# Two expert layers and an attention on one core: pairs of pages and fetches in two written orders, one picked on chip by the counts

## The chip, the cores and the metric

The kernel runs on one core of one Trainium2 chip. The metric is the device time of one execution in microseconds. The core has TensorE (PE, with its weight loads shown apart as PEld), VectorE (DVE), ScalarE (ACT), GpSimd (POOL) and SyncE (SP), which issues most DMAs. Each engine works through its own instruction queue in order and waits on semaphores for the others. A software DMA is one that POOL issues with a list of row numbers (an indirect DMA); each such instruction here moves 128 rows of 256 floats, 131 KB.

## The reference, cut to what matters

The input is x, 4 x 1024 tokens of 256 floats. Four blocks follow one another, each on a layernorm of x and added to it:

```
x = x + rwkv(layernorm(x))          # recurrence over time, per batch entry
x = x + ffn(layernorm(x))           # "layer 1" below
x = x + retention(layernorm(x))     # attention with 16 heads and a decay
x = x + ffn(layernorm(x))           # "layer 2": the same weights

def ffn(x):                          # 4096 tokens, 64 experts, width 64
    logits = x @ router_w
    scores = softmax(logits)
    topk_idx = top_k(logits + router_bias, 4)
    w = scores at topk_idx, divided by their sum
    routed = sum over the 4 picked e of w[e] * (silu(x @ wg[e]) * (x @ wu[e])) @ wd[e]
    shared = sum over 2 of (silu(x @ swg[s]) * (x @ swu[s])) @ swd[s]
    return routed + shared
```

Which expert a token picks depends on the data. The 16384 picks fill pages of 128 rows, every page for one expert; how many pages are in use after so and so many tokens is known only when the kernel runs.

## The kernel before, in words

The tokens are cut into 8 segments of 512 (`xs[i]`, held in SBUF throughout), two segments per batch entry. All work is written as lists of small steps. `track(steps, lo, hi)` gives the steps of one list evenly spread due times from lo to hi, and `merge` sorts the steps of several lists by due time and emits them; that fixes the order on each engine's queue, and a unit of due time is one pair of pages (below).

Stage 1 computes the recurrence per segment. `route(i)` has two halves. The `choose` steps (norm, logits, pick, rank, place, weigh) normalise segment i, pick experts and give each pick a row in a page; `place` keeps running page counts in `upto`. The `send` steps issue 16 indirect DMAs on POOL (L402) that write each token's normalised row to its four places in the DRAM tensor `sent`. `shared(i)` is the shared expert of segment i: TensorE L426 and L439, ACT L431, DVE L432 and L444. `plan()` works out, from `upto`, which expert owns each page. `sent` is cleared to zeros at the start, and so are the rows of `made` from pair 82 on (3584 KB, L162 to L167).

`routed()` works on pairs of pages. `step(p)` loads pair p on SP (L489: rx, 256 KB of `sent`; L491: two rw of 192 KB, the weights of the two pages' experts) and computes earlier pairs: `up(p-2)` transposes rx (L501, DVE copy L505), `mid(p-3)` does gate and up projections (L513, ACT L518, DVE L521, ACT L522), `down(p-4)` the last product (L532) and writes `made` from ACT's queue (L539). `gather(i)` brings the results of segment i back: four `fetch` steps, each of four indirect DMAs on POOL (L562), and four `add` steps, each of four DVE instructions (L573) that add the rows times their weight to `xs[i]`. The adds come LAG = 7 units after their fetches, in program order on DVE.

A fetch of segment i may run once all the pages that segment i can lie in are made. `pairs_until(i)` is the most pairs that can be in use after segment i, in the worst case of the counts: 40, 48, 56, 64, 72, 80, 88, 96. Gather i is due at `pairs_until(i) + 3.5`. MOST = 82 pairs are always computed. The other 14 are computed only if the counts need them: `rest()` loads the count into registers on all engines and puts pairs 82 to 95 in a `tc.If` (L474). Segments 6 and 7, whose `pairs_until` is above 82, are fetched behind all that, as are all steps due at 86 or later.

In layer 1 the attention runs beside the pairs: `batch(b)` is batch entry b, 41 steps over 24 units from 54 + 24 b (FIRST = 54). So entry 0 and a third of entry 1 lie before the `rest()` of layer 1 and the others behind it, together with the last gathers of layer 1 and layer 2's routes 0 to 5, two per entry, at `max(86, 54 + 24 (b + 1))` and 12 later; shared experts 0, 1 and 2 of layer 2 follow their routes (BESIDE = 3). Then come routes 6 and 7 with shared 3 and 4 as fill, layer 2's `plan()`, the pairs of layer 2 with shared 5, 6 and 7 beside them, the gathers of segments 0 to 4 and a part of segment 5, `rest()`, and the remaining gathers. As each segment is complete, SP stores it (L1146).

The pools: `xnT` (transposed normalised segments for shared experts) has 5 buffers in layer 2; `pg`, the buffers of layer 1's fetches (tag gy, 4 of them, 6 in layer 2), is held on the left to the end of the attention. Steps that the text below uses are at L392 (the exponential of the weights in `weigh`, ACT), L983, L1002 and L1006 (attention).

## Time and profile before

| what | value |
|---|---|
| median of 5 runs | 1744.22 us |
| lowest, highest | 1742.79, 1750.87 us |
| the profiled execution's own time | 1744.35 us |
| its span in the trace | 1742.6 us (1.75 us lie around it) |
| mean clock granted to TensorE | 0.88 |
| busy: PE, PEld, DVE, ACT, POOL | 1366.5, 960.9, 1021.6, 707.0, 511.5 us |
| stage 1 | 0 to about 453 us |
| layer 1's pairs | first on TensorE at 457.3 us |
| layer 1's `rest()`, skipped | TensorE's branch at 841.5 us |
| last routes (segments 6, 7) | from about 1325 us |
| layer 2's pairs | first on TensorE at 1393.1, last write of `made` issued at 1674.2 us |
| layer 2's `rest()`, skipped | TensorE's branch at 1673.2 us |
| last of 256 fetches of both layers | 1733.5 us |

How to read it: "busy" is the time in which an engine has at least one instruction at work. In a row of groups, "idle before" is the engine's idle time ahead of the group's instructions, and after "<-" stands what ended most of it. The 40 slices of the page are 43.6 us each; a digit is the busy share in tenths.

### The profile page before, as it was taken

The numbers are of one execution on the slowest core, as the hardware profiler recorded it, in microseconds if no ns is written. First come the engines' busy times: TensorE is split into PE (matmuls) and PEld (weight loads), VectorE is DVE, ScalarE is ACT, GpSimd is POOL, SyncE is SP. The second block draws the span as 40 slices with busy tenths as digits, with TensorE's granted clock in tenths as the row PEclk, the third lists the DMA queues.
The fourth block names the chain that finished last, engine by engine and source line by source line (L and its number), as shares of the span: only waits on it lengthen the run. The fifth ranks groups of instructions, "written<-read, shape, count | busy, mean of one in ns | idle before, by whom it ended". The sixth has DMA issues, their size and how long they took to land. (4 is left out here: it accounts for less than half of the span.)

```text
span 1742.6 us, 24370 instructions
## 1 busy us (share of the span) xinstructions
PE 1366.5 (78%) x8264; PEld 960.9 (55%) x8264; DVE 1021.6 (59%) x2447; ACT 707.0 (41%) x1364; POOL 511.5 (29%) x528
## 2 busy tenths in 40 slices
PE   5597999977588799989866977969689299988830
PEld 2264555554477566767532654647546178776720
DVE  5887899985255454666544842537356255554643
ACT  5675777632134443565321422224232044444310
POOL 0025043453300422231354131031130600054566
PEclk8799999988799988999776978979899699999955
DMA  9949611121699944563322010010010499999944
GB/s 367 386 144 183 176 49 49 49 87 60 231 330 335 341 155 143 177 220 96 97 75 71 22 50 27 1 49 19 31 49 7 143 307 314 327 320 310 310 154 126
DMA packets 192955, 278.15 MB, mean 160 GB/s; under 512 B 53684, under 2 KB 119095, under 8 KB 192823
## 3 DMA queue, kind: packets, MB, share of 16 engines
q1 hardware_dynamic: 144630, 166.34, 30.2%
q0 software_dynamic: 24576, 67.14, 11.8%
q10 hardware_dynamic: 23616, 43.00, 6.5%
q8 instruction: 71, 1.16, 0.3%
q14 instruction: 62, 0.50, 0.1%
HBM read 164.74 MB, written 124.26 MB: 166 GB/s over the span
## 5 line engine op out<-in xcount | busy, mean ns | idle before, releaser
L402 POOL DMA_INDIRECT sent<-xn_f,to_f x256 | 263.5, 1029 | 635.5 <-ACT w_f L392 249.0
L562 POOL DMA_INDIRECT gy_f<-made,to_f x256 | 245.2, 958 | 578.7 <-DMA rw_f<-wx 266.0
L513 PE MATMUL rg_f<-rxT_f,rw_f 128*128 128x128 f32 x1312 | 191.7, 291 | 14.6 <-DMA rw_f<-wx 4.3
L513 PEld LDWEIGHTS rg_f<-rxT_f,rw_f 128*128 128x128 f32 x1312 | 170.4, 202 | 25.1 <-DVE rxT_f L505 11.6
L505 DVE COPY rxT_f<-rt_f 128x512 f32<-128x512 f32 x164 | 112.9, 689 | 113.4 <-PE rt_f L501 86.2
L501 PE MATMUL rt_f<-ident,rx_f 128*128 128x128 f32 x656 | 110.8, 295 | 68.5 <-DMA rx_f<-sent 53.7
L532 PE MATMUL rp_f<-rw_f,rh_f 64*128 64x128 f32 x1312 | 146.1, 306 | 19.9 <-issue 6.4
L439 PE MATMUL o_f<-f_swd,sh_f 128*128 128x256 f32 x512 | 131.1, 406 | 23.4 <-DVE x L444 14.3
L573 DVE SCALAR_TENSOR_TENSOR x<-gy_f,w_f,x 128x256 f32<-128x256 f32 x256 | 120.9, 481 | 46.8 <-DMA gy_f<-made,to_f 41.2
L426 PE MATMUL u_f<-xnT_f,f_swu 128*128 128x512 f32 x256 | 128.4, 621 | 14.6 <-DVE pm L983 11.4
L532 PEld LDWEIGHTS rp_f<-rw_f,rh_f 64*128 64x128 f32 x1312 | 109.8, 193 | 49.4 <-issue 15.6
L426 PE MATMUL g_f<-xnT_f,f_swg 128*128 128x512 f32 x256 | 133.5, 639 | 3.1 <-DVE pm L983 1.5
L538 ACT COPY ry_f<-rp_f 128x256 f32<-128x256 f32 x248 | 88.2, 373 | 115.7 <-PE rp_f L532 48.0
L518 ACT ACTIVATE rs_f<-rg_f 64x256 f32<-64x256 f32 x164 | 61.5, 375 | 167.4 <-PE rg_f L513 109.7
L501 PEld LDWEIGHTS rt_f<-ident,rx_f 128*128 128x128 f32 x656 | 76.7, 148 | 92.6 <-DMA rx_f<-sent 49.8
L439 PEld LDWEIGHTS o_f<-f_swd,sh_f 128*128 128x128 f32 x512 | 101.1, 204 | 47.7 <-DVE x L444 16.7
L983 DVE TENSOR_TENSOR pm<-sc,decay 128x512 f32<-128x512 f32 x128 | 83.9, 684 | 56.9 <-remote 28.4
L521 DVE TENSOR_TENSOR rh_f<-rg_f,rs_f 64x256 f32<-64x256 f32 x164 | 69.9, 426 | 71.2 <-ACT rs_f L518 45.8
L1006 ACT COPY retT<-rp 128x256 f32<-128x256 f32 x32 | 11.9, 373 | 217.4 <-remote 116.2
L641 PE MATMUL rvk<-xnT_a,rvk 128*128 128x512 f32 x192 | 92.4, 623 | 1.0 <-DVE xnT_a L220 0.6
L426 PEld LDWEIGHTS u_f<-xnT_f,f_swu 128*128 128x128 f32 x256 | 49.5, 199 | 74.1 <-issue 58.1
L431 ACT ACTIVATE sh_f<-g_f 128x512 f32<-128x512 f32 x64 | 37.9, 597 | 116.3 <-PE g_f L426 76.5
(227 smaller groups left out, 2352.5 us busy)
## 6 DMA issues: line engine op xcount, KB each, us to landing
rw_f<-wx SPq DMA_DIRECT2D x328, 192.0 KB
rx_f<-sent SPq DMA_DIRECT2D x164, 256.0 KB
made<-ry_f ACTq DMA_DIRECT2D x164, 256.0 KB
sent<-zeros SPq DMA_DIRECT2D x7, 2048.0 KB
sent<-zeros SPq DMA_DIRECT2D x1, 10240.0 KB
x<-in_x_dram SPq DMA_DIRECT2D x8, 512.0 KB
wx<-in_wg_dram SPq DMA_DIRECT2D x2, 2048.0 KB
sent<-xn_f,to_f POOLq DMA_INDIRECT x256
```

What stands on the lines that cost most here:

```text
L402: ins = nc.gpsimd.indirect_dma_start(out=rows_sent[: pairs_until(i) * 2 * P, :], out_offset=bass.IndirectOffsetOnAxis(ap=st["to"][:, c : c ...
L426: nc.tensor.matmul(ps, lhsT=w[:, k, s], rhs=self.xnT[i][:, k, :], start=(k == 0), stop=(k == KC - 1),)
L439: nc.tensor.matmul(o[:, t, :], lhsT=st["h"][:, c, s], rhs=self.weights[2][:, c, :], start=(c == 0), stop=(c == NS - 1),)
L501: nc.tensor.transpose(tp[:, k, j, :], s["x"][:, j, k * P : (k + 1) * P], ident)
L505: nc.vector.tensor_copy(out=xT, in_=tp)
L513: nc.tensor.matmul(gu[:, j, :], lhsT=s["w"][:, j, k * 2 * F : (k + 1) * 2 * F], rhs=s["xT"][:, k, j, :], start=(k == 0), stop=(k == KC - 1),)
L532: nc.tensor.matmul(yp[:, j, :], lhsT=s["h"][r, j, :], rhs=s["w"][r, j, WD:], start=True, stop=True,)
L538: copy(out=y[:, :, c * P : (c + 1) * P], in_=yp)
L562: nc.gpsimd.indirect_dma_start(out=y[:, k, :], out_offset=None, in_=rows_made[: ready[t] * 2 * P, :], in_offset=bass.IndirectOffsetOnAxis( ...
L573: tc.keep_in_program_order(nc.vector.scalar_tensor_tensor(out=xs[i][:, t, :], in0=got[t][:, k, :], scalar=s["w"][:, c : c + 1], in1=xs[i][ ...
L641: nc.tensor.matmul(ps, lhsT=rvk[:, k, lo : lo + P], rhs=st["xnT"][:, k, :], start=(k == 0), stop=(k == KC - 1),)
L983: nc.vector.tensor_mul(out=pm, in0=ch[j]["sc"][g], in1=decay.rearrange("p (k g b) n -> p g k b n", k=KC, b=2)[:, g],)
```

## The change

- MOST, `rest()`, FIRST and ROUTE go. A second list of limits, `USUAL[i]` = 33, 38, 43, 51, 59, 67, 75, 83 pairs, stands beside `pairs_until`. `plan()` compares the page counts after each segment with 2 * `USUAL` (66, 76, 86, 102, 118, 134, 150, 166 pages; eight memsets at the start make that table) and counts how many segments exceed their limit.
- `in_order(arm)` loads that number on all engines. If it is 0, the arm written with `USUAL` runs; else the arm written with `pairs_until`. Both are in the program.
- An arm of layer 1 holds all pairs (83 with `USUAL`, 96 else), all eight gathers at `until(i) + 3.5`, and batch entries 0 and 1 from `until(0) + 14` on (47 to 71 and 71 to 95 with `USUAL`). Behind it come entry 2 with routes 0 to 3 of layer 2, 6 units apart, and entry 3 with routes 4 and 5, 12 apart; shared experts 0 and 1 follow their routes (BESIDE = 2).
- Routes 6 and 7 now have three shared experts as fill (2, 3 and 4; FILL = 3).
- An arm of layer 2 holds all pairs, all eight gathers at `until(i) + 3.5` and the stores, shared 5 and 6 from 0.5 to n - 4 and shared 7 from n - 3 to n + 11, where n is the number of pairs.
- With `USUAL`, segment 6's gather is due at 78.5 and segment 7's at 86.5, behind 83 pairs.
- `xnT` of layer 2 has 7 buffers instead of 5. `pg` moves to the right side, in the inner stack, which closes when layer 1's arm is over. The rows of `made` are no longer cleared.

```diff
--- before.py
+++ after.py
@@ -71,7 +71,8 @@
     NPAIR = (NPAGE + 1) // 2
 
 
-    MOST = min(NPAIR, (N * TOPK // P + E // 2 + 4) // 2)
+
+    USUAL = [(max(E + 2 + 10 * i, (i + 1) * SEG * TOPK // P + E // 2 + 6) + 1) // 2 for i in range(NSEG)]
 
     def seg_dram(t, i):
         b, s = divmod(i, SPB)
@@ -119,6 +120,9 @@
     nc.gpsimd.iota(pages_i, pattern=[[1, 2]], base=0, channel_multiplier=2)
     pages = const.tile([P, 2], F32, name="pages")
     nc.vector.tensor_copy(out=pages, in_=pages_i)
+    usual = const.tile([P, NSEG], F32, name="usual")
+    for i in range(NSEG):
+        nc.gpsimd.memset(usual[:, i : i + 1], 2.0 * USUAL[i])
 
     wr_sb = const.tile([P, KC, E], F32, name="wr_sb")
     rbias = const.tile([P, E], F32, name="rbias")
@@ -159,10 +163,10 @@
             got.append(t)
         return got
 
-    def clear_pages(rows, zeros, lo, hi):
+    def clear_pages(zeros, lo, hi):
 
         nc.sync.dma_start(
-            out=rows[lo * P : hi * P].rearrange("(c p) j d -> p c (j d)", p=P),
+            out=sent[lo * P : hi * P].rearrange("(c p) j d -> p c (j d)", p=P),
             in_=bc(zeros, 1, hi - lo),
         )
 
@@ -457,26 +461,34 @@
             )
             taking = self.pool.tile([P, 2], F32, tag="taking", bufs=1, name=f"taking_{self.name}")
             nc.vector.tensor_reduce(out=taking, in_=before, axis=AX.X, op=ALU.add)
-            self.used = self.pool.tile([P, 1], I32, tag="used", bufs=1, name=f"used_{self.name}")
-            nc.vector.tensor_copy(out=self.used, in_=self.upto[:, NSEG - 1, E - 1 :])
+
+            over = self.pool.tile([P, NSEG], F32, tag="over", bufs=1, name=f"over_{self.name}")
+            nc.vector.tensor_tensor(out=over, in0=self.upto[:, :, E - 1], in1=usual, op=ALU.is_gt)
+            some = self.pool.tile([P, 1], F32, tag="some", bufs=1, name=f"some_{self.name}")
+            nc.vector.tensor_reduce(out=some, in_=over, axis=AX.X, op=ALU.add)
+            self.over = self.pool.tile([P, 1], I32, tag="n_over", bufs=1, name=f"n_over_{self.name}")
+            nc.vector.tensor_copy(out=self.over, in_=some)
             self.owner = self.pool.tile([P, 2], I32, tag="plan", bufs=1, name=f"owner_{self.name}")
             nc.vector.tensor_copy(out=self.owner, in_=taking)
             nc.vector.tensor_scalar(
                 out=self.owner, in0=self.owner, scalar1=E - 1, scalar2=None, op0=ALU.bitwise_and
             )
 
-        def rest(self, pool):
+        def in_order(self, arm):
+
 
             n = nc.values_load(
-                self.used[0:1, 0:1], min_val=0, max_val=2 * NPAIR,
-                skip_runtime_bounds_check_because="place() counts at most NPAGE pages",
+                self.over[0:1, 0:1], min_val=0, max_val=NSEG,
+                skip_runtime_bounds_check_because="plan() counts segments",
             )
-            with tc.If(n > 2 * MOST):
-                merge(track(self.routed(pool, MOST, NPAIR), 0, 1))
-
-        def routed(self, pool, lo, hi):
-
-            st = {}
+            with tc.If(n < 1) as as_usual:
+                arm(lambda i: USUAL[i])
+            with as_usual.Else():
+                arm(pairs_until)
+
+        def routed(self, pool, until):
+
+            st, first, last = {}, until(0), until(NSEG - 1)
 
             def load(p):
                 nm = f"{self.name}{p}"
@@ -534,25 +546,24 @@
                             start=True, stop=True,
                         )
 
-                    copy = nc.vector.tensor_copy if c and p < pairs_until(0) else nc.scalar.copy
+                    copy = nc.vector.tensor_copy if c and p < first else nc.scalar.copy
                     copy(out=y[:, :, c * P : (c + 1) * P], in_=yp)
                 nc.scalar.dma_start(out=made[p * P : (p + 1) * P], in_=y)
 
             def step(p):
-                if p < hi:
+                if p < last:
                     load(p)
                 for d, f in ((2, up), (3, mid), (4, down)):
-                    if lo <= p - d < hi:
+                    if 0 <= p - d < last:
                         f(p - d)
 
-            return [lambda p=p: step(p) for p in range(lo, hi + 4)]
-
-        def gather(self, i, pool):
+            return track([lambda p=p: step(p) for p in range(last + 4)], 0, last + 4)
+
+        def gather(self, i, pool, until):
 
 
             nm, s = f"{self.name}{i}", self.pick[i]
-            late = pairs_until(i) > MOST
-            ready = [NPAIR if late else min(MOST, pairs_until(i) + PACE * t) for t in range(TT)]
+            ready = [min(until(NSEG - 1), until(i) + PACE * t) for t in range(TT)]
             got = {}
 
             def fetch(t):
@@ -577,14 +588,12 @@
 
             return [lambda t=t: fetch(t) for t in range(TT)], [lambda t=t: add(t) for t in range(TT)]
 
-        def gathers(self, pool, last=NSEG):
-
-            out, behind = [], MOST + 4
-            for i in range(last):
-                at = pairs_until(i) + 3.5
-                if pairs_until(i) > MOST:
-                    at, behind = behind, behind + PACE * TT
-                fetch, add = self.gather(i, pool)
+        def gathers(self, pool, until):
+
+            out = []
+            for i in range(NSEG):
+                at = until(i) + 3.5
+                fetch, add = self.gather(i, pool, until)
                 out += [track(fetch, at, at + PACE * TT), track(add, at + LAG, at + LAG + PACE * TT)]
             return out
 
@@ -609,10 +618,8 @@
         for i in range(NSEG):
             if i > 1:
                 nc.sync.dma_start(out=xs[i], in_=seg_dram(a["x"], i))
-            clear_pages(sent, zeros, done, pairs_until(i))
+            clear_pages(zeros, done, pairs_until(i))
             done = pairs_until(i)
-        if MOST < NPAIR:
-            clear_pages(made, zeros, MOST, NPAIR)
         w_neg = pa.tile([P, KC], F32, name="w_neg")
         nc.scalar.activation(out=w_neg, in_=w_t, func=AF.Exp)
         nc.vector.tensor_scalar_mul(out=w_t, in0=w_neg, scalar1=-1.0)
@@ -1082,75 +1089,80 @@
     def right(name):
         return tc.tile_pool(name=name, bufs=2, side="right", reuse_waits="tile")
 
-    BESIDE = 3
+    BESIDE, FILL = 2, 3
+    EARLY = B // 2
     BATCH = 24
-
-    FIRST = pairs_until(0) + 14
     with ExitStack() as held:
         with right("turned1") as pt, ExitStack() as inner:
             f1.turned = lambda i: pt.tile([P, KC, SEG], F32, tag="xnT", bufs=3, name=f"xnT_f1_{i}")
             with ExitStack() as own:
                 stage_1(own, f1, pf)
             pr = inner.enter_context(right("pr1"))
-            pg = held.enter_context(tc.tile_pool(name="pg", bufs=2))
+            pg = inner.enter_context(right("pg"))
             batch = stage_2(held)
-            batches = []
-            for b in range(B):
-                at = FIRST + b * BATCH
-                batches += track(batch(b), at, at + BATCH)
-            end = MOST + 4
-            steps, gathers = track(f1.routed(pr, 0, MOST), 0, end), f1.gathers(pg)
-            merge(
-                steps,
-                *([s for s in t if s[0] < end] for t in gathers),
-                [s for s in batches if s[0] < end],
-            )
-            f1.rest(pr)
+
+            def first_layer(until):
+
+                at = until(0) + 14
+                merge(
+                    f1.routed(pr, until), *f1.gathers(pg, until),
+                    *(track(batch(b), at + b * BATCH, at + (b + 1) * BATCH) for b in range(EARLY)),
+                )
+
+            f1.in_order(first_layer)
         with right("turned") as pt:
-            f2.turned = lambda i: pt.tile([P, KC, SEG], F32, tag="xnT", bufs=5, name=f"xnT_f2_{i}")
+            f2.turned = lambda i: pt.tile([P, KC, SEG], F32, tag="xnT", bufs=7, name=f"xnT_f2_{i}")
             f2.rows = (pt, 3)
             f2.weights = load_shared(
                 "f2_", lambda n, name: pt.tile([P, 4 * D], F32, tag=f"w{n}", bufs=1, name=name)
             )
             beside = []
-            ROUTE = BATCH / SPB
+            for b in range(EARLY, B):
+                at = (b - EARLY) * BATCH
+                beside.append(track(batch(b), at, at + BATCH))
+
             for i in range(NSEG - SPB):
-                b, s = divmod(i, SPB)
-                at = max(end, FIRST + (b + 1) * BATCH) + s * ROUTE
+                n = i - EARLY * SPB
+                at, step = (BATCH + n * BATCH / SPB, BATCH / SPB) if n >= 0 else (
+                    i * BATCH / (EARLY * SPB), BATCH / (EARLY * SPB)
+                )
                 choose, send = f2.route(i)
-                beside.append(track(choose + send, at, at + ROUTE))
+                beside.append(track(choose + send, at, at + step))
                 if i < BESIDE:
-                    beside.append(track(f2.shared(i), at + ROUTE, at + 1.8 * ROUTE))
-            merge(
-                *([s for s in t if s[0] >= end] for t in gathers),
-                [s for s in batches if s[0] >= end],
-                *beside,
-            )
+                    beside.append(track(f2.shared(i), at + step, at + 2 * step))
+            merge(*beside)
             held.close()
 
             last = []
             for n, i in enumerate(range(NSEG - SPB, NSEG)):
                 choose, send = f2.route(i)
-                last += [track(choose[:2], 0, 0.2), track(choose[2:], n + 0.2, n + 1), track(send, SPB, SPB + 1)]
+                last += [
+                    track(choose[:2], 0, 0.2), track(choose[2:], n + 0.2, n + 1),
+                    track(send, SPB, SPB + 1),
+                ]
             fill = []
-            for i in range(BESIDE, BESIDE + 2):
+            for i in range(BESIDE, BESIDE + FILL):
                 fill += f2.shared(i)
             merge(*last, track(fill, 1, SPB))
             f2.plan()
-            with tc.tile_pool(name="pr2", bufs=2, reuse_waits="tile") as pr:
-                side = []
-                for i in range(BESIDE + 2, NSEG):
+            pr = held.enter_context(tc.tile_pool(name="pr2", bufs=2, reuse_waits="tile"))
+
+            def second_layer(until):
+                side, stores = [], []
+                for i in range(BESIDE + FILL, NSEG - 1):
                     side += f2.shared(i)
-                gathers = f2.gathers(pr)
+                gathers = f2.gathers(pr, until)
                 for i in range(NSEG):
                     store = lambda i=i: nc.sync.dma_start(out=seg_dram(out, i), in_=xs[i])
-                    gathers.append([(gathers[2 * i + 1][-1][0] + 0.1, store)])
+                    stores.append((gathers[2 * i + 1][-1][0] + 0.1, store))
+
+                n = until(NSEG - 1)
                 merge(
-                    track(f2.routed(pr, 0, MOST), 0, end), track(side, 0.5, MOST),
-                    *([s for s in t if s[0] < end] for t in gathers),
-                )
-                f2.rest(pr)
-                merge(*([s for s in t if s[0] >= end] for t in gathers))
+                    f2.routed(pr, until), *gathers, stores, track(side, 0.5, n - 4),
+                    track(f2.shared(NSEG - 1), n - 3, n + 4 + LAG),
+                )
+
+            f2.in_order(second_layer)
 
 
 # ---- launch: one core; inputs and outputs as the reference has them ----
```

## The prediction

> **What bounds the kernel now.** First the page: busy shares, and the span in 40 slices of 43.6 us. In each window below the columns are us, busy PE, PEld, DVE, ACT, POOL (x instructions), clock granted to TensorE, DMA share, GB/s.
>
> ```profile
> PE 1366.5 (78%) x8264; PEld 960.9 (55%) x8264; DVE 1021.6 (59%) x2447; ACT 707.0 (41%) x1364; POOL 511.5 (29%) x528
> ...
> PE   5597999977588799989866977969689299988830
> ...
> POOL 0025043453300422231354131031130600054566
> ...
> DMA  9949611121699944563322010010010499999944
> ```
>
> No engine bounds it all. Stage 1 fills slices 0 to 9 and is not edited, but for a clearing. After it the limits alternate: DMA 9 (pairs of layer 1, slices 11 to 13), TensorE with dips (batches, 14 to 30), DMA 9 (pairs of layer 2, from 32), then two slices with TensorE at 0 or 3 and POOL at 6. The windows by stage, and the fetches by line:
>
> ```profile
> 500.00:525.00 25.00, 23.68 (x188) 20.33 (x189) 14.04 (x29) 10.54 (x28) 0.00 (x0) 1.00 1.00 346
> ...
> 1575.00:1600.00 25.00, 18.90 (x134) 14.90 (x132) 12.49 (x26) 9.48 (x25) 11.90 (x13) 1.00 0.88 297
> ...
> 1700.00:1725.00 25.00, 0.00 (x0) 0.00 (x0) 9.69 (x20) 0.00 (x0) 18.91 (x21) 0.50 0.49 147
> ```
> ```profile
> 450.00:600.00 150.00, 121.99 (x996) 102.78 (x996) 75.06 (x147) 58.91 (x156) 16.34 (x18) 0.96 0.93 318
> 600.00:825.00 225.00, 202.98 (x1503) 155.33 (x1504) 134.30 (x314) 113.57 (x245) 63.31 (x66) 0.93 0.53 166
> 825.00:985.00 160.00, 118.03 (x664) 76.27 (x662) 84.69 (x246) 47.33 (x91) 61.61 (x64) 0.77 0.22 68
> 985.00:1195.00 210.00, 168.30 (x997) 112.98 (x996) 96.57 (x276) 62.62 (x114) 46.13 (x48) 0.87 0.09 31
> 1195.00:1325.00 130.00, 106.38 (x747) 68.86 (x746) 67.01 (x178) 38.66 (x72) 31.05 (x32) 0.92 0.10 33
> ```
>
> Read them so. Pairs alone run at full DMA, one per 2.9 us. With POOL fetching between 1525 and 1675, a pair takes 3.97 us. At 1700 nothing but POOL and DVE works: that is a tail of fetches. In 825 to 1325 TensorE stands 107 of 500 us while POOL is busy 139: 0.77 us idle per POOL us. Last, the timeline around the two ends of layer 2's pairs, with the rows of sends (busy, mean ns, idle before and its main cause) and fetches (ns, first and last start):
>
> ```profile
> 1361.71 7.08 SPq L491 DMA_DIRECT2D rw_f<-wx  x8
> ...
> 1390.44 3.06 SPq L489 DMA_DIRECT2D rx_f<-sent  x5
> ...
> 1393.09 1.97 PE L501 MATMUL rt_f<-ident,rx_f 128*128 128x128 f32 x8 [32.15 <-DMA rx_f<-sent]
> ```
> ```profile
> 1674.21 0.33 ACTq L539 DMA_DIRECT2D made<-ry_f  x1
> ...
> 1679.77 0.95 POOL L562 DMA_INDIRECT gy_f<-made,to_f  x1 [3.06 <-SPq L474]
> ```
> ```profile
> L402 POOL DMA_INDIRECT sent<-xn_f,to_f x256 | 263.5, 1029 | 635.5 <-ACT w_f L392 249.0
> ```
> ```profile
> L562 POOL DMA_INDIRECT gy_f<-made,to_f x256: 940/946/1358, 578.3 to 1733.5; - x128
> ```
>
> TensorE stands 32 us before layer 2's pairs, while POOL sends; eight weight loads were already issued. The tail lasts from 1674.2 to 1742.6, 68.4 us: 44 fetches, one per 1.25 us (55 us), and 13 us of landing, wait, adds and the store.
>
> **Which order runs.** Counted from the inputs, the pages in use after each segment are 64, 71, 85, 97, 110, 131, 145, 158 in layer 1 and 64, 71, 84, 97, 113, 130, 146, 158 in layer 2. The limits 66, 76, 86, 102, 118, 134, 150, 166 are never passed (least margin one page), so both layers take the usual arm.
>
> **Layer 2, by parts.**
> - Tail: after the last pair only segment 7's 16 fetches remain, 28 fewer: −28 × 1.25 = −35. The 13 us around them I keep.
> - Those 28 now run beside pairs. From 1525 to 1675 there were 37.8 pairs and 85 fetches: (3.97 − 2.93) × 37.8 / 85 = 0.46 each, +12.9. Bounds: 0 if DMA had room (its share was 0.88) and +35 if nothing overlaps.
> - One pair more: +2.9.
> - Two more 512 KB stores beside pairs, at 313 GB/s 1.6 us each: +3.
> - The arm begins with a loaded count, and SP then issues rx of pair 0, which waits for the sends, ahead of any rw. The eight rw (8 × 192 KB) that went out at 1361.71 fall behind it: +4.9 at 313 GB/s, bounds 0 and +7.1 (their issue time).
> - Shared experts: three, not two, stand before the arm. By the page's rows L426 and L439 one costs (133.5 + 128.4 + 131.1) / 16 = 24.5 us of TensorE. The third goes into the 32 us hole: 0, or +24.5 if the chain of the last route leaves no hole for it. Segment 7's goes beside the tail's 16 fetches, where TensorE does nothing: 0, bound +12. Two beside pairs instead of three: pairs without any ran at the same 2.9, so 0.
> Sum −11 (bounds −35 and +20).
>
> **Layer 1 and the attention, by pieces.** The before runs 457 (first pair) to 1325 (last routes).
> - Steps 0 to 46: 47 × 2.9 = 136, 36 fetches × 0.46 = 17, lost rw loads (6 × 192 KB) 4: until 614.
> - Steps 47 to 87: 37 pairs at 2.74 us of TensorE (L501, L513 and L532 per pair: 0.68 + 1.17 + 0.89), 101, and 1.67 batches. A batch is some 87 us of TensorE, an estimate: 985 to 1325 held two batches, five routes of about 10 and three shared, (275 − 50 − 74) / 2 = 75; 600 to 840 held 31 pairs and 1.33 batches, (216 − 85) / 1.33 = 98; I take the middle. Together 246, at the 203 of 225 that 600 to 825 reached: 273, until 887.
> - Last third of batch 1, 29 us, beside 16 fetches, at the 118 of 160 of 825 to 985 or a little worse (0.66): 44, until 931. DVE's adds of segment 7 end at about 920, so the join at the arm's end costs nothing more; the next block's norms and buffers wait for those adds, which costs 11 if the batch ends first.
> - Batch 2 with four routes and two shared: 985 to 1195 held a batch, 48 sends (three routes) and three shared. A shared less and a route more is −14 of TensorE, −18 at 168 of 210; 16 sends more, each 1.27 us after the last, are 20 us of POOL, at 0.77 +15: 207. Four chains of DVE work now stand closer. If two of them (22 us each, see the first rival) lie open, it is 251; I take 225, nearer to the same stretch of before: until 1156.
> - Batch 3 with routes 4 and 5 as before, 130: until 1286.
> So −39. A second way: TensorE work −24.5 (shared) +2.7 (pair); POOL outside pairs falls from 139 to 108 (96 sends and 16 fetches at 0.96), idle −24; 18 early fetches more in the DMA-bound stretch +8, loads +4: −34. Bounds −60 (late fetches' idle all gone, the new shared order free) and +40 (next rival).
>
> **What costs nothing.** Dropping 3584 KB of zeros saves 9 us of DMA at 75 to 106, yet TensorE is busy 23.6 of 25 us from 75 on: 0, bound −9. Three more small DVE instructions in each plan stand while sends still run: 0, bound +1. Eight POOL memsets at the start: 0, bound +1. Two more xnT buffers and pg's new place only remove waits inside the blocks; the new wait they bring is the join above.
>
> The branch itself:
> ```profile
> L474 PEldq COMPARE_BRANCH  x2: 3472/3763/4054, 841.5 to 1673.2; - x2
> ```
> TensorE's two jumps took 3.8 us, the other engines' 0.05 to 0.07. Afterwards each layer has again one jump, over the other arm: 0, bounds −4 and +8.
> The Trainium skill, "Runtime: NRT & Kernel Launch", section "Instruction fetch mechanics", speaks against the change: it says that instructions are prefetched in sequence only, that a taken branch out of the window stalls until its target is fetched, and that unrolled code is better. The row above agrees for TensorE and not for the rest. By the page every engine would stall at both ends of an arm, both layers, four more times 3.8, +15; by the row it is 0.
>
> **Sum.** 1744.35 (span 1742.6 and 1.75 around it; the median of five is 1744.22) − 39 − 11 = 1694.
>
> **Rivals.**
> - Slower: the four packed routes. Each has 20 us of sends and a chain of about 22 us (segment 6's last route ran 1325 to 1347 before its first send), on engines that the batch needs in order. For it: in 1000 to 1025 TensorE did only 12.8 of 25 us during sends, and POOL's longest cause of idling, over the run, is the end of that chain. Against it: batch 3 kept 106 of 130 with two routes. If they run in series with batch 2, 4 × 42 + 87 + 49 = 304, 79 more than I count: 1773. It decides when that stretch passes 275.
> - Only layer 2 gains; the late fetches' idle time returns with packed sends, and 1325 stays: 1744 − 11 = 1733.
> - Only layer 1 gains: moved fetches cost their full 1.25, or the third shared closes the hole: 1744 − 39 + 20 = 1725.
> - The worst-case arm runs after all: 96 pairs instead of 82 in both layers, 28 × 2.9 = 81, of which the gains give back 50: 1775. Only a count that differs by a page does it.
>
> **How the numbers follow.** Forecast 0.62, alone 1665 to 1725; one layer alone 0.18 (two cases); packed routes 0.17; worst-case arm 0.03. The five runs' spread makes about 0.3% (5 us) the least that tells from no change. Slower takes the routes' and the arm's chances but for 0.01 of a mild routes' case: 0.19. Same, 0.05: 0.04 of layer two alone and that 0.01. Faster 0.76. Range 1655 to 1752: from layer 1's better bound (−60 gives 1673) less some 18 of layer 2's, up to where the routes' case begins; it leaves 0.18 above and 0.02 below.
>
> **What would show it.** Right: last made about 33 us before the end, 16 fetches behind it and TensorE busy at first; some 112 fetches among layer 2's pairs at about 4 us per pair; 83 pairs; layer 1's last fetch at about 910; batch 2 in 230 us or less. Wrong: a hole before layer 2's pairs over 40 us, pairs that slow beyond 4.3 us from pair 37 on, a join where DVE waits over 20 us with TensorE idle, or 1000 to 1150 with TensorE below half.

## The result, and the profile after

Median 1744.68 us after (44 runs) against 1746.69 us before (86 runs): ratio 1.0002, 95% interval 0.9986 to 1.0018. No change, where 50 us less were forecast. The profiled execution of the changed kernel has a span of 1734.8 us, so it lies about 8 us under its median; the stages are compared in lengths, counted from where each begins.

The page, as before in 40 slices (43.4 us here):

```profile
PE   5598999896698669889864778888798889868884
...
POOL 0022443463002233232330033321330700255545
...
DMA  9939411132799535564421011100110289979984
```

TensorE's last two slices read 8 and 4, where they read 3 and 0: the tail of layer 2 is no longer empty. But slices 20 to 22, counted from 0, read 6, 4 and 7, where they read 6, 6 and 9, and DMA, at 7 to 9 in slices 32 to 38, stays high through all of layer 2's pairs.

The tail, from the timeline of the changed kernel (start, length, what runs) and its group of fetches (smallest, median, largest ns; first and last start):

```profile
1702.84 0.33 ACTq L551 DMA_DIRECT2D made<-ry_f  x1
...
1704.75 3.62 PE L443 MATMUL o_f<-f_swd,sh_f 128*128 128x256 f32 x16
...
1725.59 0.95 POOL L573 DMA_INDIRECT gy_f<-made,to_f  x1 [0.30 <-issue]
```
```profile
L573 POOL DMA_INDIRECT gy_f<-made,to_f x256: 940/946/1398, 545.6 to 1725.6; - x128
```

The last write of `made` goes out 31.9 us before the end, TensorE works on shared 7 behind it, and the last fetch starts at 1725.6. This is what was forecast. Now the place where layer 1's arm ends:

```profile
935.31 0.42 DVE L1073 TENSOR_TENSOR x<-op,x 128x256 f32<-128x256 f32 x1 [2.46 <-PE op L1068]
...
938.19 0.42 DVE L1073 TENSOR_TENSOR x<-op,x 128x256 f32<-128x256 f32 x1 [2.46 <-PE op L1068]
938.53 5.95 DVE L584 SCALAR_TENSOR_TENSOR x<-gy_f,w_f,x 128x256 f32<-128x256 f32 x12
...
949.66 0.43 DVE L198 BATCH_NORM_STATS2 st_f<-x 128x6 f32<-128x256 f32 x1 [5.17 <-issue]
...
959.13 0.72 DVE L198 BATCH_NORM_STATS2 st_b<-x 128x6 f32<-128x256 f32 x2
...
961.93 1.18 PE L221 MATMUL tp_b<-ident,xn_b 128*128 128x128 f32 x4 [23.77 <-ACT xn_b L210]
```

The columns are start, length, instruction and, in brackets, the idle time before it and what ended it. Batch entry 1 ends with outputs that follow one another every 2.9 us, since product and addition take turns on one bank; then come twelve adds of segment 7, then 5.17 us in which DVE waits for nothing that the profile shows, then 9.5 us of norms for layer 2's routes, and only at 959.1 the norms of entry 2. TensorE stands for 23.77 us.

The table has all kernels that the text below compares. S1: start to TensorE's first work on layer 1's pairs; R: from there to layer 2's first pair; M: from there to the last write of `made`; T: from there to the end. J is a part of R: from the first product of entry 1's statistics to the first projection scaling (`qx`) of entry 2. All are us of one profiled execution. "Group" says which kernels ran on the same chip together (the recorded expectations say "call"); the ratio is to the kernel before in the same group.

| kernel | group | S1 | R | J | M | T | span | ratio, 95% |
|---|---|---|---|---|---|---|---|---|
| before | - | 457.3 | 935.7 | 11.8 | 281.1 | 68.4 | 1742.6 | 1 |
| after | - | 443.4 | 947.9 | 54.6 | 311.5 | 31.9 | 1734.8 | 1.0002 |
| e1 layer 2 only | 1 | 452.0 | 934.6 | 8.4 | 333.0 | 32.7 | 1752.3 | 1.0003 (0.9970 to 1.0036) |
| e2 layer 1 only | 1 | 452.3 | 981.3 | 54.7 | 286.4 | 68.8 | 1788.8 | 1.0119 (1.0075 to 1.0162) |
| e3 no branch | 1 | 447.7 | 941.4 | 5.4 | 314.4 | 31.9 | 1735.3 | 0.9874 (0.9823 to 0.9925) |
| e4 batches early | 1 | 446.2 | 954.6 | 69.1 | 321.8 | 32.3 | 1754.9 | 0.9988 (0.9952 to 1.0024) |
| e5 clearing kept | 2 | 443.5 | 948.1 | 54.7 | 325.0 | 32.0 | 1748.6 | 1.0112 (1.0046 to 1.0178) |
| e6 pauses | 2 | 446.0 | 946.9 | 54.7 | 320.7 | 32.8 | 1746.4 | 1.0116 (1.0051 to 1.0182) |
| e7 no branch in layer 1 | 2 | 445.7 | 924.3 | 5.4 | 311.0 | 34.2 | 1715.1 | 0.9932 (0.9884 to 0.9980) |
| e8 even due times | 2 | 443.3 | 944.4 | 54.6 | 321.3 | 39.1 | 1748.0 | 1.0126 (1.0062 to 1.0190) |
| e9 few fetches | 3 | 430.9 | 830.7 | 54.6 | 249.9 | 31.3 | 1542.7 | 0.9817 (0.9777 to 0.9857) |
| e10 layer 2 only, spaced | 3 | 426.6 | 812.1 | 11.4 | 268.0 | 32.8 | 1539.5 | 0.9849 (0.9824 to 0.9874) |
| e11 before again | 4 | 427.1 | 811.9 | 11.4 | 258.2 | 67.4 | 1564.6 | 0.9994 (0.9974 to 1.0015) |
| e12 after again | 4 | 428.0 | 828.1 | 54.7 | 272.5 | 32.3 | 1560.9 | 0.9973 (0.9952 to 0.9993) |
| e13 layer 2 only again | 4 | 426.2 | 808.1 | 11.4 | 273.8 | 32.0 | 1540.1 | 0.9887 (0.9866 to 0.9908) |
| e14 spaced again | 4 | 426.6 | 811.7 | 11.4 | 271.1 | 33.3 | 1542.7 | 0.9879 (0.9856 to 0.9901) |
| e15 as e7, again | 5 | 425.1 | 798.4 | 5.4 | 271.6 | 34.0 | 1529.1 | 0.9824 (0.9794 to 0.9854) |
| e16 join eased | 5 | 430.6 | 813.3 | 43.3 | 268.8 | 32.3 | 1545.0 | 0.9887 (0.9848 to 0.9927) |

The kernel before itself took 1757.7 and 1742.0 us in groups 1 and 2, and 1568.0, 1563.5 and 1566.4 in groups 3 to 5. Below, "first condition" means the first two rows and groups 1 and 2, "second condition" groups 3 to 5. Only kernels of one condition are compared in lengths.

From before to after, in the first condition: S1 -13.9, R +12.2, M +30.4, T -36.5, in sum -7.8. Two things were therefore to be found out: why R did not fall by 39, and what layer 2's edit is worth. S1 had to be settled first, since the dropped clearing lies in it.

### The profile page after: what moved, and what is told of

Same layout as the page of the kernel before. It is cut to its first block, busy times and chain, and to the rows that moved or that the text cites. A ratio compares the mean times of both kernels' runs of the same rounds, so it can differ in the third digit from the quotient of the medians.

```text
span 1734.8 us, 24417 instructions
## 1 busy us (share of the span) xinstructions
PE 1388.4 (80%) x8304; PEld 980.9 (57%) x8304; DVE 1023.5 (59%) x2447; ACT 697.8 (40%) x1369; POOL 517.8 (30%) x536
## 5 line engine op out<-in xcount | busy, mean ns | idle before, releaser
L406 POOL DMA_INDIRECT sent<-xn_f,to_f x256 | 267.8, 1046 | 636.0 <-issue 257.9
L525 PE MATMUL rg_f<-rxT_f,rw_f 128*128 128x128 f32 x1328 | 203.5, 299 | 26.5 <-DVE rxT_f L517 16.2
L525 PEld LDWEIGHTS rg_f<-rxT_f,rw_f 128*128 128x128 f32 x1328 | 181.4, 210 | 38.5 <-DVE rxT_f L517 22.8
L544 PE MATMUL rp_f<-rw_f,rh_f 64*128 64x128 f32 x1328 | 153.5, 317 | 35.4 <-issue 19.5
L513 PE MATMUL rt_f<-ident,rx_f 128*128 128x128 f32 x664 | 117.0, 302 | 52.0 <-DMA rx_f<-sent 31.5
L544 PEld LDWEIGHTS rp_f<-rw_f,rh_f 64*128 64x128 f32 x1328 | 116.6, 202 | 65.7 <-issue 31.5
L550 ACT COPY ry_f<-rp_f 128x256 f32<-128x256 f32 x266 | 93.8, 373 | 117.2 <-PE rp_f L544 45.1
L430 PE MATMUL u_f<-xnT_f,f_swu 128*128 128x512 f32 x256 | 124.0, 602 | 4.3 <-issue 2.5
L513 PEld LDWEIGHTS rt_f<-ident,rx_f 128*128 128x128 f32 x664 | 80.5, 152 | 80.2 <-issue 38.9
L982 PE MATMUL sc<-qx,kT 32*128 32x256 f32 x512 | 78.0, 437 | 9.9 <-ACT sh_f L435 9.5
```

Of the source, the lines that this page charges most:

```text
L406: ins = nc.gpsimd.indirect_dma_start(out=rows_sent[: pairs_until(i) * 2 * P, :], out_offset=bass.IndirectOffsetOnAxis(ap=st["to"][:, c : c ...
L430: nc.tensor.matmul(ps, lhsT=w[:, k, s], rhs=self.xnT[i][:, k, :], start=(k == 0), stop=(k == KC - 1),)
L513: nc.tensor.transpose(tp[:, k, j, :], s["x"][:, j, k * P : (k + 1) * P], ident)
L525: nc.tensor.matmul(gu[:, j, :], lhsT=s["w"][:, j, k * 2 * F : (k + 1) * 2 * F], rhs=s["xT"][:, k, j, :], start=(k == 0), stop=(k == KC - 1),)
L544: nc.tensor.matmul(yp[:, j, :], lhsT=s["h"][r, j, :], rhs=s["w"][r, j, WD:], start=True, stop=True,)
L550: copy(out=y[:, :, c * P : (c + 1) * P], in_=yp)
```

## The experiments

**One layer's part alone (e1, e2).** e1 is the kernel before with layer 2's pairs, gathers, stores and branch as in the changed one; BESIDE stays 3 and the fill 2. e2 is the changed kernel with layer 2's pairs, gathers and `rest()` as before.

```diff
 # e1, on before.py: layer 2 alone (routed_u, gathers_u: the changed versions)
-                    track(f2.routed(pr, 0, MOST), 0, end), track(side, 0.5, MOST),
-                    *([s for s in t if s[0] < end] for t in gathers),
+                    f2.routed_u(pr, until), *gathers, stores, track(side, 0.5, n - 4),
+                    track(f2.shared(NSEG - 1), n - 3, n + 4 + LAG),
...
+            f2.in_order(second_layer)
 # e2, on after.py: layer 2 as before (routed_b, gathers_b)
-            f2.in_order(second_layer)
+                f2.rest(pr)
+                merge(*([s for s in t if s[0] >= end] for t in gathers))
```

> The kernel before, with layer 2 alone written as in the changed kernel (two orders, all gathers beside the pairs, shared 7 beside the last fetches); layer 1 and the attention stay. Theory 'join' (layer 2's part gains what its trace shows, first pair to end 343.5 us against 349.5, and the loss lies at the end of layer 1's arm): 6 us faster than before, about 1740, last write of made 32 us before the end. Rival 'bursts' (denser fetches delay the hand-offs of all engines, so that layer 2 gains nothing): within 2 us of before, with pairs from first to last write of made over 312 us.

> The changed kernel with layer 2's pairs and gathers as before; layer 1, attention and routes as changed. Theory 'join': from layer 1's first pair to layer 2's first pair some 948 us (936 before), so about 12 us slower than before, 1757, with TensorE idle some 25 us between the last output of batch entry 1 and the first projection of entry 2. Rival 'the layer-1 part is neutral, the trace of the changed kernel shows a chance': within 4 us of before.

Layer 2 alone gave 1.0003: its tail fell to 32.7 us, but its pairs took 333.0 instead of 281.1. Layer 1 alone made the kernel slower, by 1.2%: R grew by 45.6, and J by 42.9, though a part of a longer J is made up behind it (e7). Between the last send and layer 2's first pair passed 18.6 us, where the changed kernel has 5.1. A late hand-off of the kind shown further below ends there (19.76 us on ACT), as one does in e3 (14.5 us), so this stretch is not charged to the change.

**The branches (e3, e7).** The worst-case arm goes, and with it the end of the block; e3 does so in both layers, e7 in layer 1 alone.

```diff
 # e3
-            with tc.If(n < 1) as as_usual:
-                arm(lambda i: USUAL[i])
-            with as_usual.Else():
-                arm(pairs_until)
+            arm(lambda i: USUAL[i])
 # e7
-            f1.in_order(first_layer)
+            first_layer(lambda i: USUAL[i])
```

> The changed kernel with the usual order written straight into the program in both layers: no count is loaded, nothing branches, and the order for worst-case counts is left out (so it serves only such counts as these inputs have). Theory 'join': the next block's work can stand beside the end of the arm, 25 to 40 us faster than the changed kernel, about 1705 to 1720. Rival 'jumps' (only the two jumps of TensorE cost): 8 us faster, 1737. Rival 'bursts': no difference beyond 4 us.

> The changed kernel with layer 1's usual order straight in the program (its order for worst-case counts left out) and layer 2's two orders as they are. Theory 'join': nearly all that both branches cost together (1.26% of before) was at the end of layer 1's arm: ratio to before 0.985 to 0.992. Rival 'jumps': each of the two branches has half of it, ratio 0.993 to 0.997.

This settles the largest part. In every kernel with layer 1's arm, whatever else was changed but for e4 and e16, J is 54.6 or 54.7; without it 5.4. R falls from 947.9 to 924.3 (944.4 to 948.1 in e5, e6 and e8), and e7 stands at 0.9932 where these three, the kernels with the arm in the same group, stand at 1.011 to 1.013. The branch of layer 2 shows no price: M is 311.0 with it (e7) and 314.4 without (e3), T 34.2 and 31.9.

**Batches earlier (e4).** If the join costs because entry 1 ends last, entry 1 should end sooner. In this kernel the attention's first steps read some rows before layer 1's last additions to them.

```diff
-                at = until(0) + 14
+                at, BATCH = until(0) + 12, 21
```

> The changed kernel with the two batch entries of layer 1's arm due 2 units earlier and over 21 units instead of 24 (45 to 66 and 66 to 87 instead of 47 to 71 and 71 to 95), so that entry 1 ends with the pairs. Theory 'join': its eight outputs, which stood alone for 20 us, now stand beside pairs, 8 to 15 us faster than the changed kernel. Rival 'TensorE is the limit of that stretch': what is drawn forward only delays the pairs, within 4 us of the changed kernel.

Entry 1's statistics came 27 us earlier (440.8 us after the first pair instead of 467.5), but J grew to 69.1: the arm still ends with segment 7's fetches and adds, and nothing of entry 2 can be brought ahead of them. Entry 2 began 12 us earlier, R was no shorter (954.6), and the ratio is 0.9988. So the price is that of a closed block, not of entry 1 being late.

**The clearing (e5).** The rows of `made` from pair 82 on are cleared again.

```diff
+        nc.sync.dma_start(
+            out=made[82 * P : NPAIR * P].rearrange("(c p) j d -> p c (j d)", p=P),
+            in_=bc(zeros, 1, NPAIR - 82),
+        )
```

> The changed kernel with the clearing of the last 14 pairs of made (3584 KB of zeros) put back at its old place. Five profiles so far begin layer 1's pairs at 457.3, 452.0 and 452.3 us with that clearing and at 443.4, 447.7 and 446.2 us without. Theory 'clearing': it begins at 452 to 457 again and the whole is about 8 us slower than the changed kernel. Rival 'chance, or another part of the change': it begins at 443 to 448 and the whole is the same.

S1 is 443.5 with the clearing and 443.4 without, and the ratio (1.0112) is that of e6 and e8, which have none. e2, which has it too, took 452.3. So the 13.9 us by which the profiled execution of the changed kernel was ahead at its first pair are not shown to be the clearing's: in the first condition S1 is 443.5 to 457.3 with it and 443.3 to 447.7 without, in the second 426.2 to 427.1 with it and 425.1 to 430.9 without.

**Fewer or thinner fetches beside layer 2's pairs (e6, e8, e10, e14, e9).** Theory: fetches issued back to back slow the pairs, and spacing helps. e6 was to put a POOL memset behind each fetch of segments 0 to 6, e8 spreads the gathers' due times evenly over the pairs, e10 and e14 space those of e1 by 7 pairs a segment, with limits on the read rows that move with them. e9 leaves out the fetches and adds of segments 0 to 6 in layer 2.

```diff
 # e6
+                    if self.name == "f2_" and i + 1 < NSEG:
+                        rest = pool.tile([P, 512], F32, tag="rest", bufs=1, name=f"rest_{nm}_{c}")
+                        nc.gpsimd.memset(rest, 0.0)
 # e8
+                if self.name == "f2_":
+                    at = max(at, until(0) + 3.5 + PACE * TT * i)
 # e10, e14, on e1
-                at = until(i) + 3.5
-                fetch, add = self.gather_u(i, pool, until)
+                at = max(until(i), until(0) + 7 * i) + 3.5
+                fetch, add = self.gather_u(i, pool, until, int(at - 3.5))
 # e9
+                if self.name == "f2_" and i + 1 < NSEG:
+                    fetch, add = [lambda: None] * TT, [lambda: None] * TT
```

> The changed kernel with a POOL memset of 0.5 us after each of layer 2's fetches for segments 0 to 6, so that fetches are 1.8 us apart and not 1.25. Theory 'bursts' (POOL's fetches one straight behind the other delay the hand-offs between the other engines): layer 2's pairs, first transposition to last write of made, take under 300 us instead of 311 to 333, 10 us or more faster in all. Rival 'volume' (only the bytes and the number of fetches count): 311 us or more, no gain, or up to 10 us slower since fetches come later.

> The changed kernel with layer 2's gathers in the usual order due every 8 units from 36.5 on (36.5, 44.5, ... 92.5) instead of 36.5, 41.5, 46.5, 54.5, ... 86.5: never more than two fetches to a pair, but 12 more fetches behind the last pair. Theory 'density' (where 2.7 fetches stand to a pair each costs some 0.85 us, at two to a pair 0.5 to 0.6): pairs 285 to 295 us, the tail 15 us longer, 5 to 15 us faster in all. Rival 'the same price for each': pairs 8 us shorter, the tail 15 longer, 7 us slower.

> The changed kernel without the 112 fetches and the adds of segments 0 to 6 in layer 2 (their routed part is left out of the output; pairs, shared experts, stores and segment 7's gather stay). Layer 2's pairs took 311 to 333 us in the kernels with its usual arm and 281 in the one before. Theory 'fetches' (the fetches beside the pairs cost all of what a pair takes above 2.85 us, 0.67 to 0.86 us each): pairs 237 to 250 us. Rival 'arm' (branch code, stores, lost weight loads and the shared experts take a good part): pairs over 265 us.

> The kernel of layer 2 alone (layer 1 and attention as before the change), with the gathers of the usual order due every 7 units from 36.5 to 85.5 and 86.5, and each fetch bound to wait for the pair that stands there, so that POOL can't run ahead: 2.3 fetches to a pair throughout, the same 16 behind the last pair. Before, due times alone didn't hold POOL back. Theory 'density': pairs 290 to 305 us instead of 333, 15 us or more faster than before the change. Rival 'the same price for each fetch wherever it stands': pairs 311 to 333, no faster than layer 2 alone was, ratio to before 0.997 to 1.003.

The theory found no support, but it was hardly tested. e6 has no pauses. Nothing in its edit holds a memset in place, and the trace has all 112 in one stretch ahead of layer 2's first fetch:

```profile
1388.63 65.14 POOL L580 MEMSET rest_f<- 128x512 f32 x112
1507.46 0.98 POOL L573 DMA_INDIRECT gy_f<-made,to_f  x1 [53.69 <-DMA rx_f<-sent]
```

The fetches stayed 1.25 us apart (median), as in the changed kernel. So e6 says nothing on pauses; it is one more run of nearly the changed kernel (M 320.7, ratio as e5). In e8 only 13 fetches instead of 24 were out by pair 40, but 41 by pair 48, where the changed kernel has 44: a due time holds back the order of the queue, but POOL then runs on as soon as its fetch is ready. M stayed at 321 and the tail grew to 39. e10 came out at 0.9849 and looked like the cure of e1's 1.0003; but the kernel before took 1568 us in that group, so another condition had to be ruled out.

**Four kernels in one group (e11 to e14).** Unchanged repeats: before, after, e1, e10.

> The kernel before, unedited, for a profile beside the next three on the same chip. In the last two kernels' profiles no wait was ended by 'remote' (an update that no recorded instruction or DMA accounts for); in the profile of before there were 273 us of such waits, in that of the changed kernel 203. Theory 'late hand-offs' (these waits are a condition of the chip at the time, not of the kernel): here before and the three others have them all or have none of them; without them before takes about 1568 us.

> The changed kernel, unedited. Theory 'join and dense fetches' alone: ratio to before 0.998 to 1.004, as first measured, whatever the condition of the chip. Theory 'late hand-offs': if there are no 'remote' waits here, the fetches beside layer 2's pairs cost 0.35 to 0.5 us each and not 0.67 to 0.86, its pairs take under 285 us, and the ratio is 0.985 to 0.995; if there are such waits, 0.998 to 1.004.

> Layer 2's part alone, as in the first of these experiments (ratio 1.0003). Theory 'late hand-offs': without 'remote' waits its pairs take under 285 us instead of 333 and the ratio is 0.980 to 0.990; with them 0.997 to 1.003. Theory 'density': pairs over 300 us and no gain in either condition.

> Layer 2's part alone with the fetches held to 2.3 a pair, as in the last call (ratio 0.9849, pairs 268 us, no 'remote' waits). Theory 'density': 10 us or more faster than the kernel of layer 2 alone in this same call. Theory 'late hand-offs': in a condition without 'remote' waits it is within 4 us of it; with them it may be anything up to 15 us faster.

Spaced and unspaced fetches are equal here (0.9879 and 0.9887, intervals almost the same; by pair 56, 49 fetches are out in e14 and 56 in e13), so e10's result was the condition, not the spacing. Whether more spacing would help where e1 ran, no run shows. e12's pairs took less than 285 us, as the theory of late hand-offs had it, but its ratio of 0.9973 missed the expected 0.985 to 0.995: the end of layer 1's arm costs as much here (e15). What differs between the conditions is seen in the groups. The copies of the attention, before (first condition), then e11, the same kernel: busy and mean ns, then the idle time ahead and what ended it.

```profile
L1006 ACT COPY retT<-rp 128x256 f32<-128x256 f32 x32 | 11.9, 373 | 217.4 <-remote 116.2 <-PE rp L1002 91.5 <-PE rp_f L532 9.7
```
```profile
L1006 ACT COPY retT<-rp 128x256 f32<-128x256 f32 x32 | 11.9, 371 | 106.1 <-PE rp L1002 106.1
```

The profile writes "remote" where it finds no instruction of this core that released the wait when it ended. Such waits sum to 273 us in before, 203 in after and 333 in e1, and none is listed in e9, e11, e12, e13 or e15. One of them close up, in the changed kernel, at the shared experts that fill the last routes:

```profile
1367.66 3.62 PE L443 MATMUL o_f<-f_swd,sh_f 128*128 128x256 f32 x16
...
1376.99 0.69 DVE L448 TENSOR_TENSOR x<-o_f,x 128x512 f32<-128x512 f32 x1 [8.36 <-remote]
1377.73 5.99 PE L443 MATMUL o_f<-f_swd,sh_f 128*128 128x256 f32 x16 [6.45 <-DVE x L448]
...
1386.15 0.96 POOL L406 DMA_INDIRECT sent<-xn_f,to_f  x1 [0.30 <-issue]
...
1391.12 0.69 DVE L448 TENSOR_TENSOR x<-o_f,x 128x512 f32<-128x512 f32 x1 [13.44 <-remote]
```

And the same place in e12, the same kernel:

```profile
1232.33 3.62 PE L443 MATMUL o_f<-f_swd,sh_f 128*128 128x256 f32 x16
...
1235.98 0.69 DVE L448 TENSOR_TENSOR x<-o_f,x 128x512 f32<-128x512 f32 x1 [2.69 <-PE o_f L443]
1236.73 3.72 PE L443 MATMUL o_f<-f_swd,sh_f 128*128 128x256 f32 x16 [0.79 <-DVE x L448]
```

TensorE's product ends at 1371.3 in the one and DVE begins at 1377.0; in the other the hand-off takes 0.03 us. Most of the late time lies where POOL issues sends or fetches back to back: 87% of it in before and 77% in the changed kernel, while such stretches (three or more, less than 1 us apart) fill 37 and 38% of the span. They are not enough to bring it on, since POOL issues the same way in e12. So there is a condition, of the chip or of the time, in which hand-offs between engines come late. Like profiles are 174 to 212 us longer in it (after and e12, e1 and e13). The runs don't show that the late hand-offs make up all of that, and I found nothing in the kernels that brings the condition on or ends it. What causes it stays open.

It decides what layer 2's edit is worth. Without late hand-offs layer 2 changed, from e11 to e13, by M +15.6 and T -35.4, and the kernel took 1.1% less; with them M grew by 30 to 52 (after, e1), and the gain was 6 us in one profile and a loss of 16 in the other. The 112 fetches beside the pairs cost (272.5 - 249.9) / 112 = 0.20 us each without late hand-offs, by e12 and e9. An estimate with them, from the same floor, is (311.5 - 249.9) / 112 = 0.55, and 0.74 in e1.

**The join, again and eased (e15, e16).** e15 is e7 in the other condition. e16 keeps both arms of layer 1, holds the norms of entry 2 ahead of those of routes 0 to 3, and lets segment 7's adds follow their fetches sooner.

```diff
 # e16
-            nc.vector.bn_stats(out=st, in_=xt)
+            ins = nc.vector.bn_stats(out=st, in_=xt)
+            if i[:2] == "b2" or i in ("f2_0", "f2_1", "f2_2", "f2_3"):
+                tc.keep_in_program_order(ins)
...
+                lag = 5.0 if self.name == "f1_" and i + 1 == NSEG else LAG
```

> Layer 1's usual order straight in the program, as before, now on a chip that shows (as in the last call) no 'remote' waits. Theory 'join': the statistics of batch entry 1 come 399 us after layer 1's first pair, the first projection of entry 2 some 5 us after them instead of 55, entry 2 takes up to 20 us longer; layer 1's first pair to layer 2's 790 to 805 us instead of 828; ratio to before 0.975 to 0.985. Rival 'what the join hides comes back later' (the routes' sends bound the stretch): 820 us or more, ratio 0.993 or more.

> The changed kernel with the norms of batch entry 2 held ahead of those of layer 2's routes 0 to 3 on VectorE (the 16 norms of the routes took 9.5 us at the start of the block, before entry 2's first). Theory 'join': the gap from entry 1's statistics to entry 2's first projection falls from 55 to 44 to 48 us, and the whole by 5 to 9 us against the changed kernel (ratio to before 0.992 to 0.995 where it was 0.9973). Rival 'TensorE waits for the routes then': the gap falls, the whole does not.

The windows around the join: us, busy PE, PEld, DVE, ACT, POOL (x instructions), granted clock, DMA share, GB/s. First e12, then e15:

```profile
835.00:850.00 15.00, 12.42 (x27) 6.84 (x28) 3.87 (x9) 0.00 (x0) 2.71 (x3) 0.50 0.12 35
850.00:865.00 15.00, 3.62 (x8) 1.70 (x7) 6.40 (x14) 0.00 (x0) 0.00 (x0) 0.50 0.32 107
865.00:880.00 15.00, 1.79 (x6) 1.10 (x7) 13.30 (x59) 5.49 (x14) 0.00 (x0) 0.50 0.00 1
```
```profile
835.00:850.00 15.00, 13.86 (x49) 10.02 (x49) 9.09 (x29) 9.62 (x19) 7.15 (x8) 0.79 0.25 75
850.00:865.00 15.00, 13.56 (x64) 8.69 (x63) 12.95 (x35) 0.84 (x2) 0.00 (x0) 0.89 0.01 3
865.00:880.00 15.00, 13.85 (x83) 10.07 (x81) 5.94 (x21) 7.04 (x14) 0.00 (x0) 0.54 0.29 104
```

With the arm, TensorE does 27 matmuls in the first window, with a granted clock of 0.50, then 14 in 30 us. Without it, entry 2's steps run between entry 1's outputs, and TensorE works through all three windows. R is 798.4 in e15 against 828.1 in e12: the arm's end costs 30 us here and 24 in the first condition. J comes in four pieces: entry 1's statistics and outputs alone (from 911 to 938 in the changed kernel), the adds (6), the gap (5) and the norms of other work ahead (9.5). e16 took the last piece and a part of the adds: J is 43.3, R 813.3, and its ratio 0.9887, where 0.992 to 0.995 were expected, with an idle time of 11.46 us on TensorE in place of 23.78 (e12):

```profile
869.08 0.43 DVE L198 BATCH_NORM_STATS2 st_b<-x 128x6 f32<-128x256 f32 x1 [4.50 <-issue]
...
871.67 1.18 PE L223 MATMUL tp_b<-ident,xn_b 128*128 128x128 f32 x4 [11.46 <-ACT xn_b L212]
```

e16 and e13 both keep the worst case in every place and beat the kernel before by 1.1% in the second condition; against the changed kernel e13's ratio is 0.9914 by the medians of their group (0.9887 and 0.9973). e15 is faster still (0.9824), but it has no order for the worst case in layer 1. e16 was not run in the first condition.

## Why the prediction was wrong, by its steps

- **Which order runs: right.** 83 pairs in each layer; the usual arm ran.
- **Layer 2's tail: right.** -35 was forecast; T fell by 36.5 and, without late hand-offs, 35.1. Behind the last write of `made` 46 fetches stood in before and 18 in the changed kernel, 28 fewer, as forecast.
- **Layer 2's pairs: the size off, inside its bounds.** +24 was forecast; M grew by 30.4 in the first profiles and 14.3 in the second condition. The price of a moved fetch, 0.46 us, rests on 85 fetches in before's window; the window's row has 79 on POOL, all of them fetches:

```profile
1525.00:1675.00 150.00, 127.47 (x836) 104.31 (x834) 82.59 (x163) 60.61 (x160) 75.52 (x79) 0.90 0.89 298
```

  With 79 the prediction's own sum gives 0.50 each, and +14 for the 28. That is near the estimate of 0.55 for the changed kernel in the same condition, below the 0.74 of e1 and far above the 0.20 without late hand-offs: the price is no constant. The pace was right on average, with 4.0 us a pair from pair 40 on, but not even: pairs 30 to 50 took 4.6 each. In sum layer 2 gave -6 (first profiles) or -21 (e11 to e12), for -11. The bounds stated for that sum, -35 and +20, are not what the bounds of its terms add up to (-29 and +50); both results lie inside either.
- **The third shared expert in the hole: right.** Layer 2's first pair follows the last send after 5.1 us in the changed kernel, as in before (5.2), and entry 3's last output after 69.3 us in both.
- **"DVE's adds of segment 7 end at about 920, so the join at the arm's end costs nothing more": wrong, and this step failed the forecast.** The pieces of R, cut where an entry's last output ends (in before at 982, 1187 and 1324 us, where the prediction has 985, 1195 and 1325):

| us | before | forecast | after | e7 no arm | e11 before | e12 after | e15 no arm |
|---|---|---|---|---|---|---|---|
| first pair to entry 1's end | 524.7 | 474 | 495.2 | 495.3 | 477.0 | 426.6 | 432.0 |
| entry 1's end to entry 2's | 205.0 | 225 | 248.1 | 225.7 | 155.8 | 220.5 | 188.0 |
| entry 2's end to entry 3's | 136.7 | 130 | 135.3 | 133.9 | 110.9 | 111.6 | 108.9 |
| entry 3's end to layer 2's first pair | 69.3 | 68 | 69.3 | 69.3 | 68.2 | 69.4 | 69.5 |

  The join stands in the second row: 248.1 us with the arm's end and 225.7 without it, where 225 were forecast, and 220.5 and 188.0 in the other condition. So a term put at 0, with a bound of 11, cost 22 to 32 us. The bound counted only the adds' delay. The adds were late, at 501 us after the first pair (944.5) and not 463 (920), since in DVE's queue twelve of them stand behind entry 1's last output; but in e7 they ended at 509 and entry 2 ran beside them. What the prediction left out is that a block ends for all engines: in before entry 1's serial outputs overlapped with entry 2 (its first scaling is at 966.2 us, entry 1's last output at 982.0) and cost nothing, and here nothing was left to overlap. The sign that the prediction named for this, TensorE idle for over 20 us at a join, is there (23.77); only DVE waited for 5 of them and spent most of the others on the adds and on norms for later. Its sign of being right, batch 2 in 230 us or less, is not there.
- **The end of entry 1: a second error, 21 us, that the join does not make.** It came 495 us after the first pair, for 474, in the changed kernel and in e7 alike. Some 14 of the 21 were there when the last pair was made (444.5 for 430). In the second condition it came 50 (e12) and 45 us (e15) earlier than in before, for 51. So the error is large only where hand-offs come late; which wait makes it, no run takes apart. Without the join R would have been -11 (e7 against before) or -13.5 (e15 against e11), not -39; in e15 about half of the shortfall lies in entry 2 (188.0 - 155.8 = 32, for 20).
- **The branch: the weight was put on the wrong row.** The prediction took the 0.05 us of the jump's row on DVE as its cost. In the changed kernel the rows still read so:

```profile
L484 PEldq COMPARE_BRANCH  x4: 77/1688/3855, 423.8 to 1709.2; - x4
L484 DVEq COMPARE_BRANCH  x4: 47/53/61, 427.6 to 1728.4; - x4
```

  But the next instruction of DVE, which waits for nothing, begins 5.17 us after the adds (also in e12; 4.50 in e16), and no such gap stands there in e7 and e15, which have no jump. On TensorE the stall is in the row (3.3 us at the end of layer 1's arm, 3.9 at layer 2's), on DVE in the gap behind it. That the gap is the jump's is read from where it stands and where it is absent; no row names its cause. In before, DVE was idle for only 0.43 us at its jump over `rest()`:

```profile
842.64 1.00 DVE L573 SCALAR_TENSOR_TENSOR x<-gy_f,w_f,x 128x256 f32<-128x256 f32 x2 [0.43 <-DVEq L474]
```

  That jump passes 14 pairs with two DVE instructions each (L505, L521), while the one at the end of the usual arm passes the whole worst-case arm, with 96 pairs and 128 adds. The Trainium skill, "Runtime: NRT & Kernel Launch", section "Instruction fetch mechanics", says that a taken branch stalls where its target lies outside the prefetched window, until that has been fetched; a short jump at 0.43 us and a long one at 4.5 to 5.2 agree with it for DVE too, though no run varied the length alone. The prediction preferred the row to the rule, and the row was the wrong place to look. Its +15 by the page was no better: it counted a stall at both ends of an arm, and the branch at the start of the usual arm is not taken (0.08 and 0.10 us on TensorE). The gap is one of the four pieces of J, 5 of some 49 us.
- **The dropped clearing: 0 was forecast,** and no cost of it shows (e5).
- **The rivals.** None was this case. "Only layer 2 gains" comes nearest, but by another mechanism: layer 1 had no gain because the join and a late entry 1 took it away. Where the arm's end is absent, the packed routes did not stretch entry 2 beyond the forecast in e7, and by 12 us at most in e15, far from the 79 of that rival. One reading for them was wrong: POOL's longest cause of idling in before is the loads of the pairs' weights (266.0 us, 4 waits), and the end of the routes' chain comes second (249.0). That the whole came out so near to no change is chance. In the profiles the -7.8 us are S1 -13.9, which no edit explains, R +12.2 and layer 2 -6.1; with late hand-offs M alone ranges from 311 to 333.

## What to carry to other kernels

A block that ends in a branch closes every queue: what ended serially under the cover of the next work lies open, so look at what runs last in it on each engine, and what the next block puts first. Read the stall of a taken jump in the gap to the engine's next instruction, not in the jump's own row. After writing a pause or a due time, look in the trace whether it stands where it was written. And when a kernel's time differs by a tenth between groups of runs, repeat the comparison of the old kernels in one group before believing a new cure.

## What was not expected of the hardware

The same program took 1742 to 1758 us in some groups and 1564 to 1568 in others, on one core. In the slower ones some hand-offs from one engine to another came late (40 in before and 45 in the changed kernel, half of them or less over 5 us, the longest 24.5), most of them while POOL issued indirect DMAs back to back. The record gives the same chip number for groups 1 to 3, of which the first two had this and the third had not, so a chip's number alone does not tell. In e3 one late hand-off held DVE for 20.38 us just ahead of layer 2's pairs:

```profile
1379.68 0.69 DVE L448 TENSOR_TENSOR x<-o_f,x 128x512 f32<-128x512 f32 x1 [20.38 <-remote]
```

The gain of layer 2's edit is 1.1% in the one condition and not to be measured in the other (e13 and e1, the same program). What brings this condition on was not found.
